# Graph attention with a gated FFN on one Trainium2 core: when scan results are transposed back, and when the first node's destination terms are copied

## The chip, the core and the metric

The kernel runs as one program on 1 core of a Trainium2 chip. The metric is device time in microseconds (us) of one execution, from its own record. Five engines run their own instruction lists in order and meet through semaphores: PE (TensorE; PEld is its weight load), DVE (VectorE), ACT (ScalarE), POOL (GpSimd) and SP (SyncE, which here only issues DMA).

## The reference

One layer of a relational graph attention network, then a feed-forward network with four experts, of which two count per node.

```python
feat_all = einsum('ni,rhid->rnhd', layernorm(x), conv_weights)   # 30000 nodes, 8 relations, 4 heads, 64
feat_src_e = feat_all[edge_type, src]                            # 510000 edges, sorted by dst
e = leaky_relu(sum(feat_src_e * attn_l[edge_type], -1) + sum(feat_all[edge_type, dst] * attn_r[edge_type], -1))
m = segment_max(e, dst)
ex = exp(e - m[dst])
alpha = ex / segment_sum(ex, dst)[dst]
x = x + segment_sum(alpha[..., None] * feat_src_e, dst).reshape(30000, 256) + h_bias
x = x + ffn(layernorm(x))      # shared 256-256-128-256, plus the 2 best of 4 experts 256-128-64-256, by a softmax gate
```

All data are float32. The edges come sorted by destination, 17 per node on average.

## The kernel before

**Two stages.** The first stage (up to about 1800 us) computes the features of every node and relation and stores them in DRAM, and works out lists and records of the edges. The second stage (about 1800 us to the end) is the one that the change touches. A third part, a slow path for unusual graphs, has loops that run zero times here.

**Blocks.** The second stage goes through 253 blocks of edges (`t` from 0 to 252; 2048 edges each, as 128 partitions x 16 units, neighbours overlapping). A block's feature rows are partly read back from a staged array and partly fetched by indirect DMAs from POOL (`gather`, L1152, 12 to 13 per block). Each block belongs to at most 128 nodes.

**What a block goes through.** By the names in the code:

- `dest_nodes` (DVE, L1164) makes a one-hot matrix, `dest_rows_of` (PE, L1172) multiplies it with the nodes' destination terms into PSUM tile `pe`: for each partition the terms of up to 4 nodes that its edges can belong to.
- `dest_first` (ACT, L1177) copies the first node's terms from `pe` to all 16 units of the tile `ere`. `dest_next` (DVE, L1182, three instructions) overwrites them where a unit belongs to the second, third or fourth node. `dest_types` (DVE, L1189) picks the relation.
- `scores` (DVE, L1206 to L1213) adds source and destination terms and takes the maxima `tops` of runs within a partition.
- `turn_ends` (PE, L1219) transposes `tops` into PSUM tile `t1`. `across` (DVE, L1225 and L1226) runs two scans over the partitions and writes the maxima of neighbours into `car`. `turn_back` (PE, L1232) multiplies `car` with a small constant and so fetches the scan results back, transposed, into PSUM tile `t2`. `t1` and `t2` share one PSUM buffer.
- `softmax` (DVE, L1238 to L1243) reads `t2` and subtracts the maxima; `exps` (ACT, L1248 and L1249) takes the exponentials and copies them beside the features.
- `onehot` (ACT, L1199 and L1200, three units at a time) makes the one-hot matrices of edges to nodes; `weigh` (DVE, L1256) multiplies features by exponentials; `sums` (PE, L1263) adds up per node; `finish` (DVE, L1329 to L1333) divides and adds the input. `keep` stores the rows.

**The experts.** Finished nodes go through the feed-forward network in groups of 512 (`Experts`). A group's work is a list of 23 steps, one of which is issued in each slot (below): normalise (`spread` L918 with a table load on ACT, `scale` L928), transpose (`turn`, PE L936, copied out on ACT L938 as `xT`), the gate (L944), the first, second and third layers (L1000, L1047, L1068 to L1071). What follows a step on ACT or DVE is issued one slot later, as `after`. A group begins in every fourth block, and at times in the fifth.

**The order is written out by hand.** Under `tc.manual_schedule()` (L1338) nothing reorders instructions: a loop over `t` and over six slots `c` issues everything, and each engine runs its part in that order. In iteration `t`, by slot:

- slot 0: DMAs of block `t+3`, gathers of `t+1`, store of `t-3`; `weigh` of `t-2`; `softmax` and `exps` of `t-1`
- slot 1: `scores` of `t`; `dest_first` of `t+1`, behind the experts' step and its `after`
- slot 2: `turn_ends` of `t`; two `dest_next` of `t+1`
- slot 3: `across` of `t`, the third `dest_next`, `dest_nodes` of `t+2`
- slot 4: `turn_back` of `t`; `finish` of `t-2`
- slot 5: `dest_rows_of` of `t+2`; `dest_types` of `t+1`
- in every slot: one chunk of `weigh` and, at the end, one experts' step with the former step's `after`, one chunk of `onehot` of `t-1` and one chunk of `sums` (of `t-2` in slots 0 to 2, of `t-1` in slots 3 to 5).

## Time and profile before

| what | value |
|---|---|
| median of 3 runs | 6114.72 us (6105.19 to 6117.77) |
| profiled execution, own time | 6111.61 us |
| its span (first to last instruction) | 6109.9 us |
| PE busy | 5621.0 us, 92% |
| PEld busy | 3559.5 us, 58% |
| DVE busy | 4519.3 us, 74% |
| ACT busy | 3396.1 us, 56% |
| POOL busy | 3983.9 us, 65% |
| mean granted TensorE clock | 0.954 of full speed |

The profiled execution is 3.1 us under the median of the runs, and its time is 1.7 us over its span. Shares of busy time are means over both stages. From 2300 to 5900 us the second stage runs evenly: in each 400 us PE is busy for 360 to 370 us, DVE for 353 to 357, ACT for 272 to 279, POOL for 289 to 296. All four engines are in use most of the time and wait for one another in turn, so the time is read from who waits for whom inside a block, and not from these shares.

### The profile page before, as it was taken

The page shows a single profiled execution, that of the slowest core. Times are in us where ns is not written, and L with a number is a line of the kernel's source. Part 1 is how long each engine was busy: PE and PEld are TensorE (multiplying, and loading weights), DVE is VectorE, ACT ScalarE, POOL GpSimd, SP SyncE. Part 2 cuts the span into 40 slices and gives each one's busy share as a digit, 9 for nine tenths or more (in the row PEclk, how much of TensorE's full clock was granted, in tenths as well). Part 3 has the DMA queues.
Part 4 walks back from the last instruction along what each step waited for, and adds up shares of the span by engine and source line. Part 5 has one row for each costly group of instructions (what it writes and reads, how often), then busy time and mean ns, then how long its engine had stood idle before and what let it go on. Part 6 is the DMA issues. An engine that isn't in the chain of part 4 may idle for free. (4 is left out here: it accounts for less than half of the span.)

```text
span 6109.9 us, 88666 instructions
## 1 busy us (share of the span) xinstructions
PE 5621.0 (92%) x20369; PEld 3559.5 (58%) x20370; DVE 4519.3 (74%) x13102; ACT 3396.1 (56%) x8847; POOL 3983.9 (65%) x4455
## 2 busy tenths in 40 slices
PE   8899999999987999999899999889999989999997
PEld 4455555555545666666666666666666666666664
DVE  6575333333339888888888888888898888888883
ACT  3343222222226667667666676767666666666763
POOL 1035666666666777777777777777777777777770
PEclk9999999999998999999999999999999999999998
DMA  8568999999997666666666666666666666666651
GB/s 193 137 243 274 355 364 358 356 356 354 356 321 208 179 182 182 184 184 177 180 183 181 182 180 182 181 181 178 182 189 180 181 180 180 182 178 180 184 169 35
DMA packets 847971, 1315.89 MB, mean 215 GB/s; under 512 B 226577, under 2 KB 646053, under 8 KB 817221
## 3 DMA queue, kind: packets, MB, share of 16 engines
q1 hardware_dynamic: 587476, 710.74, 35.5%
q0 software_dynamic: 194400, 539.40, 31.4%
q10 hardware_dynamic: 65552, 59.93, 3.0%
q8 instruction: 169, 2.77, 0.2%
q14 instruction: 374, 3.06, 0.2%
HBM read 855.54 MB, written 454.06 MB: 214 GB/s over the span
## 5 line engine op out<-in xcount | busy, mean ns | idle before, releaser
L1152 POOL DMA_INDIRECT ft<-feat,rk x3154 | 3021.0, 958 | 1133.5 <-issue 418.2
L1263 PE MATMUL po<-ft,oh 128*128 128x260 f32 x8100 | 2181.3, 410 | 23.6 <-ACT oh L1200 22.9
L1263 PEld LDWEIGHTS po<-ft,oh 128*128 128x128 f32 x8100 | 1546.4, 200 | 609.7 <-issue 255.2
L368 PE MATMUL ps<-w,xT 128*128 128x448 f32 (+1 forms) x4700 | 1717.3, 520 | 25.4 <-ACT fo L370 16.6
L1199 ACT ACTIVATE oh<-icol,rk 128x128 f32<-128x128 f32 x4050 | 1333.6, 390 | 0.0
L368 PEld LDWEIGHTS ps<-w,xT 128*128 128x128 f32 x4700 | 875.8, 191 | 723.3 <-issue 606.7
L1256 DVE TENSOR_TENSOR ft<-ft,p 128x768 f32<-128x768 f32 x1518 | 1285.6, 855 | 5.1 <-ACT ft L1249 5.0
L803 POOL DMA_INDIRECT fr<-feat,lists x896 | 851.1, 950 | 428.1 <-issue 235.1
L370 ACT COPY fo<-ps 128x448 f32<-128x448 f32 (+1 forms) x830 | 427.6, 521 | 1203.4 <-PE ps L368 850.6
L1200 ACT ACTIVATE oh<-oh 128x384 f32<-128x384 f32 x1518 | 740.3, 488 | 49.3
L1182 DVE COPY_PREDICATED ere<-rk,pe 128x512 f32<-128x512 int16 (+1 forms) x759 | 554.0, 730 | 187.6 <-ACT ere L1177 170.8
L1248 ACT ACTIVATE p<-e 128x64 f32<-128x64 f32 (+1 forms) x253 | 71.1, 281 | 796.9 <-DVE e L1243 796.4
L370 DVE COPY fo<-ps 128x256 f32<-128x256 f32 x345 | 180.0, 522 | 440.8 <-PE ps L368 415.0
L1000 PE MATMUL ph<-xT,v 128*128 128x512 f32 (+2 forms) x960 | 450.6, 594 | 0.8 <-ACT h L1001 0.8
L357 DVE COPY xT<-ptr 128x256 f32<-128x256 f32 x170 | 71.9, 423 | 319.3 <-PE ptr L355 319.1
L1189 DVE COPY_PREDICATED ere<-rk,ere 128x256 f32<-128x256 int16 (+1 forms) x759 | 247.0, 325 | 17.5
L1000 PE MATMUL ph<-xT,w 128*128 128x512 f32 (+2 forms) x480 | 259.2, 666 | 0.0
L1232 PE MATMUL t<-ways,car 36*128 36x8 f32 x506 | 98.4, 265 | 174.7 <-DVE car L1226 174.7
L1070 PE MATMUL pf<-v,a 128*128 128x256 f32 x940 | 243.8, 382 | 4.9 <-DVE a L1055 4.9
L1000 PEld LDWEIGHTS ph<-xT,v 128*128 128x128 f32 x960 | 175.1, 193 | 124.1 <-issue 114.2
L1232 PEld LDWEIGHTS t<-ways,car 36*128 36x128 f32 x506 | 77.8, 192 | 267.6 <-issue 262.9
L1001 ACT ACTIVATE h<-ph,b 128x512 f32<-128x512 f32 (+2 forms) x180 | 121.0, 672 | 197.7 <-PE ph L1000 190.5
(241 smaller groups left out, 5806.9 us busy)
## 6 DMA issues: line engine op xcount, KB each, us to landing
feat<-fo SPq DMA_DIRECT2D x234, 1040.0 KB
ft<-stage SPq DMA_DIRECT2D x160, 390.0 KB
stage<-fr SPq DMA_DIRECT2D x448, 130.0 KB
stage<-fr ACTq DMA_DIRECT2D x448, 130.0 KB
ft<-feat,rk POOLq DMA_INDIRECT x3154
ft<-stage SPq DMA_DIRECT2D x80, 520.0 KB
xt<-in_x_dram SPq DMA_DIRECT2D x253, 128.0 KB
x_d<-xt SPq DMA_DIRECT2D x252, 128.0 KB
```

What stands on the lines that cost most here:

```text
L368: nc.tensor.matmul(ps, t["xT"][:, k, :], w[:, k, c0:c1], start=k == 0, stop=k == 1)
L370: eng(t["fo"][:, h0:h1, :HD], ps[:, :n].rearrange("p (a d) -> p a d", d=HD))
L803: nc.gpsimd.indirect_dma_start(out=fr, out_offset=None, in_=feat[0:min(early(i // GI * GI) * P, N) * R, :], in_offset=bass.IndirectOffsetO ...
L1000: nc.tensor.matmul(ps[:, :self.w], lhs, rhs, start=i == 0, stop=i == len(pairs) - 1)
L1070: nc.tensor.matmul(pf[:M], self.a2[:, i, tok], v3[:, i, :], start=False, stop=False)
L1152: nc.gpsimd.indirect_dma_start(out=s.ft[:, u].rearrange("p h d -> p (h d)"), out_offset=None, in_=feat[:, :], in_offset=bass.IndirectOffse ...
L1182: nc.vector.copy_predicated(s.ere, s.mask[:, k - 1, :, None].to_broadcast(at), s.pe[:, k:k + 1].to_broadcast(at))
L1189: nc.vector.copy_predicated(s.ere[:, :, :n], s.bits[:, i, :, None].to_broadcast([P, s.u, n]), s.ere[:, :, n:2 * n])
L1199: nc.scalar.activation(s.oh[:, u, :], icol, AF.Abs, bias=s.nd[:, u:u + 1])
L1200: nc.scalar.activation(s.oh[:, u0:u1], s.oh[:, u0:u1], AF.Relu, bias=1.0, scale=-1.0)
L1256: nc.vector.tensor_mul(fc, fc, pc[:, :, None].to_broadcast([P, (u1 - u0) * H, HD]))
L1263: nc.tensor.matmul(s.po.rearrange("n h d -> n (h d)"), s.oh[:, u, :], s.ft[:, u].rearrange("p h d -> p (h d)"), start=u == 0, stop=u == s. ...
```

## The change

`turn_back` of a block is issued in slot 5 in place of slot 4. On PE it so comes after the experts' step and the chunk of `sums` of slot 4, and just ahead of `dest_rows_of`. `dest_first` of the next block is issued in slot 0 in place of slot 1. On ACT it so comes ahead of the `onehot` chunk of slot 0 and ahead of the `after` of slot 1. No instruction is added or taken away, none has another shape, and no DMA is moved.

```diff
@@ -1356,7 +1356,7 @@
                             nc.sync.dma_start(*outs.pop(0))
                     if c == 2:
                         at(turn_ends, t)
-                    if c == 4:
+                    if c == 5:
                         at(turn_back, t)
                     if c == 5:
                         at(dest_rows_of, t + 2)
@@ -1388,7 +1388,7 @@
                                 late.append(after)
                         for after in ready:
                             after()
-                    if c == 1:
+                    if c == 0:
                         at(dest_first, t + 1)
                     at(onehot, t - 1, c)
                     at(sums, t - 1 - (c < 3), (c - 3) % NCH)
```

## The prediction

> **What bounds the kernel now.** The chain that ended last on the page holds only an idle loop's instruction, so I read the waits of the steady part (2100 to 5900 us): waiting instruction, releaser, total us, times, longest.

> ```profile
> ACT p L1248 <- DVE e L1243: 708.9, 225, 9.1
> ...
> DVE ere L1182 <- ACT ere L1177: 160.2, 107, 2.2
> PE t L1232 <- DVE car L1226: 159.7, 70, 2.8
> ...
> DVE car L1225 <- PE t L1219: 95.5, 120, 1.9
> ```

> The second and third are the two waits that the change goes for. Each falls in few blocks, so I followed the timeline block by block. The experts' 23 steps give a cycle of four kinds of block: norm (holds L918, L928, L936), gate (L944, then the first layer), expert (second layer), last (L1068 to L1071). Between the start of the run and its end I count 55 cycles from one norm block to the next: 38 of four blocks, 17 with one more block, without experts' steps, behind the last block. One norm block, first on DVE, then PE, then ACT (start, us, engine, line, operation, idle time before it and releaser):

> ```profile
> 4110.57 0.94 DVE L1256 TENSOR_TENSOR ft<-ft,p 128x768 f32<-128x768 f32 x1
> 4113.09 1.49 DVE L1182 COPY_PREDICATED ere<-rk,pe 128x512 f32<-128x512 int16 x2 [1.58 <-ACT ere L1177]
> ```

> ```profile
> 4111.65 1.58 PE L1263 MATMUL po<-ft,oh 128*128 128x260 f32 x6 [0.63 <-ACT oh L1200]
> 4116.03 0.36 PE L1232 MATMUL t<-ways,car 36*128 36x8 f32 x2 [2.80 <-DVE car L1226]
> 4116.32 0.66 PE L936 MATMUL ph<-ident,c_xn 128*128 128x128 f32 x4
> 4116.81 2.36 PE L1263 MATMUL po<-ft,oh 128*128 128x260 f32 x6
> ```

> ```profile
> 4107.91 0.28 ACT L1248 ACTIVATE p<-e 128x64 f32<-128x64 f32 x1 [8.00 <-DVE e L1243]
> ...
> 4112.49 0.56 ACT L1177 COPY ere<-pe 128x512 f32<-128x512 f32 x1
> ...
> 4120.91 1.28 ACT L1248 ACT_TABLE_LOAD   x1
> 4123.30 0.28 ACT L1248 ACTIVATE p<-e 128x64 f32<-128x64 f32 x1 [1.10 <-DVE e L1243]
> ```

> DVE sets the pace here: PE waits for it for 2.80 us, and ACT for 8.00 us before and 1.10 us behind a stretch without a gap. In the gate block PE then waits for xT from ACT (L938, 1.48 us at 4124.42). From there through the expert block to L1219 of the last block PE has no wait, and DVE waits for PE at L1225 (0.7 to 0.9 us in each expert block, 0.2 to 0.8 in each last one). So a cycle is: DVE from the last block's L1225 to the gate block's L1243, ACT's L1248, L1249, L938, then PE.

> The TensorE clock belongs to PE's part. Four stretches (us, busy PE PEld DVE ACT POOL with counts, granted clock, DMA share, GB/s):

> ```profile
> 4113.90:4117.30 3.40, 1.27 (x9) 1.22 (x10) 3.36 (x7) 3.34 (x10) 2.49 (x4) 0.99 0.37 94
> 4117.30:4120.70 3.40, 3.40 (x13) 2.92 (x12) 3.26 (x12) 3.30 (x10) 2.49 (x4) 0.50 0.84 187
> ...
> 4188.90:4192.30 3.40, 2.12 (x17) 2.06 (x18) 3.30 (x8) 3.12 (x10) 2.56 (x3) 1.00 0.58 176
> 4192.30:4195.70 3.40, 3.40 (x9) 1.66 (x8) 3.19 (x9) 2.36 (x8) 2.72 (x3) 0.51 0.41 104
> ```

> A stretch of 3.41 us with little streamed through PE is followed by one at half clock: the first pair lies in the norm block, behind the 2.80 us wait, where PE has time; the second in the gate block, behind the xT wait and the 4-column L944, where PE has none. Cycles of four blocks last 65.77, 67.39 and 69.02 us with 0, 1 and 2 half-clock stretches in PE's part, so each costs 1.62 us. Over the 55 cycles they are none in 24, one in 21, two in 10: 41 in all, 66 us.

> **dest_first one slot earlier.** No instruction is added: 253 copies of 0.57 us. In the norm block the copy can start at 4110.17, behind L918, and end at 4110.7; DVE is free at 4111.51, so its wait of 1.58 us goes. Over 55 norm blocks these waits are 89.1 us. But DVE is then met by ACT. ACT works without a gap from 4107.91 to the end of the table load at 4122.19, and the order inside does not change its sum. So L1248 at 4123.30 can come earlier only by its own wait, 1.10 us (1.056 mean, 58.1 us over 55), and with it xT and PE's part. I take 58 and not 89.

> The other 75 us of that wait lie in expert blocks (0.6 to 2.2 us each). There L1225 comes next and waits for PE: its 0.91 us becomes up to 2.8. Worth nothing, as PE's part has no gap.

> What the copy is moved past: `onehot` chunk 0 comes 0.57 us later. In the norm block PE's 0.63 us wait for it becomes 1.20, hidden by the 2.80 us wait behind; without that cover 0.57 x 55 = 31 us. Elsewhere PE uses that chunk only in slot 3, microseconds after it is made. No DMA or POOL instruction is issued from the moved lines.

> **turn_back one slot later.** 253 times two matmuls, 0.39 us. In the norm block PE no longer stands 2.80 us for `car`: it goes to L936, which needs ACT's second pair of L928 (end 4115.48), so it starts at 4115.5 in place of 4116.32 and reaches `turn_back` about 1.9 us later, when `car` (now ready near 4114.3) has long been there. This saves PE time before the xT wait, which ACT ends: worth nothing directly.

> The cost is in DVE, which needs the result for L1238. Such a wait is absent from the trace; its size follows from these starts at the end of a gate block (the third is the expert block that follows):

> ```profile
> 4070.50 0.18 DVE L1238 TENSOR_TENSOR c<-t,rk 128x32 f32<-128x32 f32 x1
> ```

> ```profile
> 4067.84 0.39 PE L1232 MATMUL t<-ways,car 36*128 36x8 f32 x2
> 4071.29 0.38 PE L1172 MATMUL pe<-er,ohb 128*128 128x128 f32 x2
> ```

> ```profile
> 4080.31 0.41 DVE L1225 TENSOR_TENSOR_SCAN car<-through,t 4x127 f32<-4x127 f32 x1 [0.91 <-PE t L1219]
> ```

> The result lands 2.27 us before L1238 wants it; the new place ends where L1172 starts, 3.06 us later. So L1238 waits about 0.8 us. 31 of the 55 gate blocks are like this (mean 0.81, 25 us in all); in the others there are 3.7 us to spare. Queued behind L1238 are DVE's `scores` and the whole expert block, and ACT's L1248, but DVE has 0.91 + 1.9 us to spare there before L1225, and what PE needs of ACT (the second layer's input) is 6 us ahead. So I cost it at nothing, and at 25 us if that cover is gone. At the end of the last block 1.35 us of 1.81 are used, of the expert block 3.06 of 3.42, of the norm block about 2.6 of 5.2: no wait.

> **The clock.** The norm block's hole in PE, 0.63 + 2.80 us around three sums, becomes about 1.2 and 1.8: it trips the half clock less often. That sounds good, but a norm block at full clock brings PE to the xT wait sooner. In the 10 cycles without a half-clock stretch there the xT wait is 3.1 us in place of 1.4, and all 10 have two half-clock stretches in PE's part. With xT 1.1 us earlier the wait would be about 2. Bounds: all 41 stretches go (-66 us), or every cycle has two (110 - 41 = 69, +112 us). I take one per cycle, 55 - 41 = 14 more, +23 us, between the two kinds of row.

> [...] The rows above trip on a gap of 2.80 us and on 1.46 us of waiting beside 4-column matmuls. [...]

> **Sum.** 6111.6 (profiled execution) - 58 + 23 = 6076.6; the median lies 3.1 above it: 6080. POOL sets a floor: it stands idle beyond its usual 0.3 us per gather for only 130 us over the blocks from the 15th on, so no more than about 130 us can be won.

> **Rivals.**

> - *The clock's stretches shrink.* xT comes earlier and PE's holes are shorter, so PE's part may see fewer: from 6057 (still 41) to 6114.7 - 58 - 66 = 5991 (none). For it: 24 cycles have none now. Against: the 10 cycles with a fast norm block.
> - *Half clock in PE's part, twice per cycle (slower).* If the norm block now always runs at full clock, the xT wait and L944 fill a stretch in each cycle: 6114.7 - 58 + 112 = 6169. It decides from 36 more stretches on (58 / 1.62), 1.4 per cycle. For it: those 10 cycles, all with two. Against: their xT wait was 3.1 us, not 2.
> - *The gain is spent elsewhere.* L1238's 25 us and the 31 us of the later one-hot chunk are not covered: 6114.7 - 58 + 56 = 6113. Against: 2.8 us of room on DVE in the expert block and the hole on PE in the norm block.
> - *The waits only change their names:* ACT is the limit at once and 0 of the 58 is left, 6115. Against: the 1.10 us wait is there in all 55 cycles.

> **How the numbers follow.** About 0.2% (12 us) is what a measurement of this kernel can tell from no change. Forecast (6057 to 6100) 0.45; fewer stretches 0.25; gain spent or only renamed 0.14; two stretches per cycle, or well on the way there, 0.16. Faster by over 0.2% are the first two and a little of the third: 0.72; within 0.2%: 0.13; slower: 0.15. The range goes down to the middle of the second case, 6024, and up through the third to a quarter of the last, 6125.

> **What would show it.** Right: L1182's wait for L1177 nearly gone (from 160 us to under 20), L1232's for L1226 under 30, L1225's for L1219 up to some 170 as expert blocks wait for PE in its place; L1248 behind the norm block without its 1.1 us; L1238 with a new wait for L1232 of some 25 us; cycles of 64.7, 66.3 or 67.9 us. Wrong: an L1182 wait that stays; a norm block whose ACT stretch grows beyond 14.3 us; an L1238 wait after which L1225 of the expert block no longer waits; or cycles of four blocks mostly at 67.9 us or above, which would be the clock.

## The result, and the profile after

| | us |
|---|---|
| before, median of 7 runs | 6113.95 (6097.06 to 6117.77) |
| after, median of 7 runs | 6138.55 (6134.09 to 6143.47) |
| ratio after / before, 95% interval | 1.0047 (1.0035 to 1.0059) |
| after, profiled execution, its span | 6136.24, 6134.5 |

The change makes the kernel 24.6 us slower. The profiled executions differ by the same 24.6 us (6136.24 against 6111.61), so they can be compared part by part.

The waits of the steady part, kernel after (2100 to 5900 us; waiting instruction, releaser, total us, times, longest):

```profile
ACT p L1248 <- DVE e L1243: 695.3, 174, 8.4
...
DVE car L1225 <- PE t L1219: 235.8, 153, 2.2
...
PE pg L944 <- ACT xT L938: 135.0, 53, 2.6
...
DVE c L1238 <- PE t L1232: 53.9, 69, 1.6
...
PE ph L936 <- ACT c_xn L928: 52.0, 87, 1.1
```

The line of the kernel before for xT, same view:

```profile
PE pg L944 <- ACT xT L938: 85.2, 47, 3.3
```

Of the two waits that the change went for, L1182's for L1177 (160 us before) is gone, and L1232's for L1226 (160 us before) is down to 4.9 us. In their place L1225 waits 236 us for PE in place of 95, L1238 has a wait that it did not have, and PE waits for xT in every cycle (135 us in place of 85). The kernel got rid of two waits in the norm block, and PE comes later to the blocks behind it.

One norm block with the start of its gate block, timeline of the kernel after, first ACT, then PE (start, us, engine, line, operation, idle time before it and releaser):

```profile
4178.27 0.28 ACT L1248 ACTIVATE p<-e 128x64 f32<-128x64 f32 x1 [8.00 <-DVE e L1243]
...
4191.26 1.28 ACT L1248 ACT_TABLE_LOAD   x1
4192.55 0.28 ACT L1248 ACTIVATE p<-e 128x64 f32<-128x64 f32 x1
```

```profile
4185.40 0.33 PE L936 MATMUL ph<-ident,c_xn 128*128 128x128 f32 x1 [1.10 <-ACT c_xn L928]
...
4186.05 1.48 PE L1263 MATMUL po<-ft,oh 128*128 128x260 f32 x6
4187.46 0.39 PE L1232 MATMUL t<-ways,car 36*128 36x8 f32 x2
...
4190.73 0.28 PE L944 MATMUL pg<-gw,xT 128*128 128x4 f32 x2
4193.62 3.15 PE L944 MATMUL pg<-gw,xT 128*128 128x4 f32 x14 [2.60 <-ACT xT L938]
```

ACT's L1248 behind the norm block starts without its wait of 1.1 us, as forecast, and ACT is the limit there now. PE's hole of 2.80 us ahead of L1232 has gone: L936 and six matmuls of `sums` come first. But PE then reaches L944 early and stands 2.60 us for xT. The same place by stretches of 3.40 us (us, busy PE PEld DVE ACT POOL with counts, granted clock, DMA share, GB/s):

```profile
4183.90:4187.30 3.40, 2.13 (x11) 1.40 (x9) 3.29 (x11) 3.34 (x10) 2.67 (x3) 1.00 0.45 113
4187.30:4190.70 3.40, 3.40 (x20) 2.96 (x19) 3.26 (x10) 3.34 (x10) 2.60 (x3) 1.00 0.93 222
4190.70:4194.10 3.40, 0.80 (x6) 0.68 (x5) 3.23 (x8) 3.31 (x8) 2.49 (x4) 0.92 0.83 280
4194.10:4197.50 3.40, 3.40 (x15) 3.30 (x16) 2.97 (x8) 2.83 (x9) 2.70 (x3) 0.50 0.46 120
4197.50:4200.90 3.40, 3.40 (x9) 1.83 (x9) 1.20 (x3) 1.14 (x4) 2.58 (x3) 0.58 0.41 102
4200.90:4204.30 3.40, 3.40 (x11) 1.85 (x11) 3.16 (x12) 1.43 (x5) 2.49 (x4) 1.00 0.48 125
```

The first row is the norm block's hole, now too full to bring a half-clock stretch: the second row stands at 1.00. The third row is the xT wait with PE busy for 0.80 of 3.40 us. Two stretches at half clock follow, not one. Most of the first is L944 itself: 14 of its 16 matmuls, of 4 columns each, keep PE "busy" for 3.15 us and stream 56 columns in all, and the second half-clock stretch follows.

**Where the 24.6 us are.** The second stage is cut into the same 55 cycles as before. PE's part of a cycle runs from L944 of the gate block to L1219 of the last block, and a half-clock stretch is one step of 3.413 us at 0.50 in the clock's own records.

| half-clock stretches in PE's part | cycles before | cycles after | us, four blocks, before / after | us, five blocks, before / after |
|---|---|---|---|---|
| none | 24 | 0 | 65.77 / - | 80.09 / - |
| one | 21 | 12 | 67.39 / 66.31 | 81.78 / 80.62 |
| two | 10 | 43 | 69.02 / 67.90 | 83.36 / 82.24 |

Cycles of one kind are 1.1 us shorter, as forecast. But the kinds have changed: 98 stretches (12 + 86) in place of 41, each at 1.6 us. 55 x 1.056 = 58 us are won and 57 x 1.62 = 92 us lost, +34; the mean cycle says 71.41 to 71.99, +0.58 x 55 = +32 us. The other -7 us lie outside these cycles, 6.3 of them ahead of the 15th block's softmax (2032.59 before, 2026.31 after); what they come from stays open.

The length of the xT wait does not settle alone whether a cycle has one stretch or two: after the change 12 cycles with a wait of 2.5 to 2.6 us have one, and 40 with 2.3 to 2.6 us have two. In the traces of before and after every change of the clock lies on a fixed grid of 3.413 us. In the 12 cycles PE restarts behind the xT wait 0.66 to 2.13 us after a line of this grid, in all 43 others outside that range. Ahead of PE's part half clock costs nothing that shows: in the kernel before, four-block cycles with no stretch in PE's part have 2.7 such stretches there in the mean, those with two have none, and 1.62 us for each one in PE's part fits both.

### The profile page after: what moved, and what is told of

It reads as the page before. It is cut to its first block, busy times and chain, and to the rows that moved or that the text cites. A ratio compares the mean times of both kernels' runs of the same rounds, so it can differ in the third digit from the quotient of the medians.

```text
span 6134.5 us, 88626 instructions
## 1 busy us (share of the span) xinstructions
PE 5660.2 (92%) x20369; PEld 3558.2 (58%) x20370; DVE 4519.3 (74%) x13102; ACT 3398.0 (55%) x8847; POOL 3988.0 (65%) x4455
## 5 line engine op out<-in xcount | busy, mean ns | idle before, releaser
L1263 PE MATMUL po<-ft,oh 128*128 128x260 f32 x8100 | 2154.2, 407 | 60.1 <-ACT oh L1200 45.2
L1263 PEld LDWEIGHTS po<-ft,oh 128*128 128x128 f32 x8100 | 1545.3, 200 | 656.2 <-issue 237.5
L1256 DVE TENSOR_TENSOR ft<-ft,p 128x768 f32<-128x768 f32 x1518 | 1286.1, 855 | 2.4 <-ACT ft L1249 2.4
L1200 ACT ACTIVATE oh<-oh 128x384 f32<-128x384 f32 x1518 | 740.3, 488 | 48.1
L1182 DVE COPY_PREDICATED ere<-rk,pe 128x512 f32<-128x512 int16 (+1 forms) x759 | 552.4, 728 | 21.1 <-ACT ere L1177 4.4
L1248 ACT ACTIVATE p<-e 128x64 f32<-128x64 f32 (+1 forms) x253 | 71.1, 281 | 804.9 <-DVE e L1243 804.3
L944 PE MATMUL pg<-gw,xT 128*128 128x4 f32 x940 | 162.7, 296 | 143.6 <-ACT xT L938 143.6
L1225 DVE TENSOR_TENSOR_SCAN car<-through,t 4x127 f32<-4x127 f32 x253 | 101.6, 402 | 251.0 <-PE t L1219 250.7
L1000 PE MATMUL ph<-xT,w 128*128 128x512 f32 (+2 forms) x480 | 271.6, 694 | 0.0
L944 PEld LDWEIGHTS pg<-gw,xT 128*128 128x128 f32 x940 | 163.0, 255 | 152.7 <-ACT xT L938 149.4
```

What stands on the lines that cost most here:

```text
L944: nc.tensor.matmul(pg[:M, t, :], self.xT[:, k, t * M:(t + 1) * M], gw[:, k, :], start=k == 0, stop=k == 1)
L1000: nc.tensor.matmul(ps[:, :self.w], lhs, rhs, start=i == 0, stop=i == len(pairs) - 1)
L1182: nc.vector.copy_predicated(s.ere, s.mask[:, k - 1, :, None].to_broadcast(at), s.pe[:, k:k + 1].to_broadcast(at))
L1200: nc.scalar.activation(s.oh[:, u0:u1], s.oh[:, u0:u1], AF.Relu, bias=1.0, scale=-1.0)
L1256: nc.vector.tensor_mul(fc, fc, pc[:, :, None].to_broadcast([P, (u1 - u0) * H, HD]))
L1263: nc.tensor.matmul(s.po.rearrange("n h d -> n (h d)"), s.oh[:, u, :], s.ft[:, u].rearrange("p h d -> p (h d)"), start=u == 0, stop=u == s. ...
```

## The experiments

Two theories. **Clock:** the freed waits move PE's idle time from the norm block, where half clock costs nothing, to the xT wait, where it costs 1.6 us a stretch. **Late fetch:** `turn_back` one slot later makes DVE late at L1238 (53.9 us of waits) and the cycle with it. A kernel's ratio is to the kernel before, run on the same chip, with its 95% interval. Except where "after" is named, the edits are made to the kernel before.

### One half of the change at a time

`e1_turn_back_only`:

```diff
-                    if c == 4:
+                    if c == 5:
                         at(turn_back, t)
```

> Only turn_back moves (slot 5); dest_first stays in slot 1. Clock theory (the new order closes PE's hole in the norm block, PE comes sooner to the wait for xT, and PE's part of the cycle gets more half-clock stretches of 1.62 us): the 58 us of the earlier copy are missing, L1248 behind the norm block keeps its 1.05 us wait, cycles stay at 65.8 or 80.1 us plus 1.62 per stretch, and there are 60 to 110 stretches in place of 41: 6145 to 6225 us. Late-fetch theory (the loss is DVE's new wait for turn_back at L1238, 54 us in the steady part of the changed kernel): 41 stretches or so, L1238 waits for 25 to 54 us, and the cycles are longer by that: 6140 to 6195 us.

`e2_dest_first_only`:

```diff
-                    if c == 1:
+                    if c == 0:
                         at(dest_first, t + 1)
```

> Only dest_first moves (slot 0); turn_back stays in slot 4. Clock theory: cycles of 64.7 or 79.05 us plus 1.62 per half-clock stretch; PE's wait for car in the norm block falls from 2.8 to about 0.7 us, PE then waits for c_xn some 1.1 us, so the norm block is mostly at full clock here too and PE's part has 70 to 98 stretches: 6100 to 6148 us. Late-fetch theory: no wait at L1238, 41 stretches, 6114 - 58 = 6056 us.

Measured: e1 6198.78 us, ratio 1.0153 (1.0139 to 1.0166); e2 6146.01 us, ratio 1.0060 (1.0046 to 1.0073). Waits of e1, then of e2 (2100 to 5900 us):

```profile
PE pg L944 <- ACT xT L938: 181.2, 52, 4.0
...
DVE ere L1182 <- ACT ere L1177: 142.5, 104, 1.6
```

```profile
DVE car L1225 <- PE t L1219: 291.7, 156, 3.5
...
PE pg L944 <- ACT xT L938: 151.6, 53, 3.0
```

e2 has the old `turn_back` and no wait of L1238 at all, and is slower all the same, with 105 half-clock stretches in PE's part. So late fetch falls as the cause. Its four-block cycles of 66.35 us (one stretch) and 67.89 us (two) are those of the kernel after. In e1 the L1182 wait and ACT's 1.06 us stay, so nothing is won: its four-block cycles last 67.39 us with one stretch, as before, 68.96 with two and 69.90 with three, of which the first begins while PE still stands for xT. That makes 108 stretches in place of 41, or the worth of about 100 if only what lies behind the xT wait is counted. L1238's waits (40.8 us in e1) do not show in the cycles with one stretch. Either half alone is enough to bring PE to the xT wait early. Put together they lose less than e1 alone because the 58 us of `dest_first` are real.

### Filling the xT wait

`e3_fill_xT_wait` is the kernel after with three matmuls that compute nothing, into a tile that nobody reads, ahead of L944 (the trace shows each as two records):

```diff
+if todo and getattr(todo[0], "__name__", "") == "gates":
+    hole = ph_p.tile([P, TM], F32, name="ph")
+    for _f in range(3):
+        nc.tensor.matmul(hole, ident, v1.rearrange("p e k f -> p (e k f)")[:, :TM], start=True, stop=True)
```

> The changed kernel with three more matmuls (identity by 512 columns of the first experts' weights, into an unread PSUM tile) issued on PE ahead of the gate matmuls L944, 3 x 0.86 us in the 2.6 us wait for xT. Clock theory: the idle window before PE's part is gone, 98 half-clock stretches fall to 0 to 30, and 1.62 us come back for each: 5980 to 6030 us. Late-fetch theory, or any in which the waits themselves cost the time: unchanged or slower by what does not fit in the wait, 6138 to 6160 us.

Measured: 5984.12 us, ratio 0.9795 (0.9782 to 0.9809). PE on the timeline, then the stretches (columns as above); L1388 is the filling:

```profile
2937.99 2.36 PE L1263 MATMUL po<-ft,oh 128*128 128x260 f32 x10
2940.18 2.74 PE L1388 MATMUL ph<-v,ident 128*128 128x512 f32 x6
2942.76 1.97 PE L944 MATMUL pg<-gw,xT 128*128 128x4 f32 x16
```

```profile
2939.40:2942.80 3.40, 3.40 (x13) 1.85 (x11) 3.16 (x11) 3.31 (x8) 2.48 (x4) 1.00 0.69 228
2942.80:2946.20 3.40, 3.40 (x24) 2.89 (x23) 3.30 (x7) 3.34 (x10) 2.49 (x4) 1.00 0.42 113
```

No wait of L944 for L938 is left, and of the 98 stretches in PE's part none. The cycles last 64.72 and 79.04 us: 1.05 us less than before's undisturbed 65.77 and 80.09, which is the gain that the prediction gave to `dest_first` (1.056 us). The mean granted clock of the whole run goes from 0.953 to 0.979. More work on PE, all of it useless, makes the kernel 2.5% faster than it was with the change alone.

### Real work in its place

`e4_sums_before_gate` is the kernel after with two chunks of `sums` (those of slots 1 and 2) issued ahead of the gate's matmuls; nothing is added:

```diff
+if c == 1 and t < NBLK and todo and getattr(todo[0], "__name__", "") == "gates":
+    for i in range(2):
+        at(sums, t - 2, 4 + i)
+        ahead_of_gate.append(1 + i)
...
+if c in ahead_of_gate:
+    ahead_of_gate.remove(c)
+else:
     at(sums, t - 1 - (c < 3), (c - 3) % NCH)
```

> The changed kernel, where in slot 1 of a gate block the sums chunks of slots 1 and 2 (5 units, 2.6 us of PE) are issued ahead of the gate matmuls, so that PE works while it waits for xT. Clock theory: PE's part is 2.6 us shorter in each cycle (143 us over 55) and loses most of its half-clock stretches (up to 90 us); POOL's floor and DVE cut this off: 5970 to 6020 us. Late-fetch theory: L1238 comes later on DVE or as before, 6110 to 6140 us.

Measured: 5956.02 us, ratio 0.9754 (0.9740 to 0.9767), 14 us below the range that was expected. It beats both kernels; e11 (below) cannot be told from it, and nothing in this study is faster. Its waits (2100 to 5800 us):

```profile
POOL ft L1152 <- issue: 334.2, 1097, 0.3
POOL ft L1152 <- PE po L1263: 226.7, 744, 0.3
...
DVE e L1206 <- DMA ft<-feat,rk: 62.2, 56, 3.3
...
PE pg L944 <- ACT xT L938: 22.5, 52, 1.4
```

35 stretches remain in PE's part. Ahead of a gather POOL no longer waits longer than 0.5 us for anything, and nearly always 0.3 us, its usual gap (before: up to 3.5 us); DVE now waits 62 us for the gathered rows at L1206, in place of 1.0 us before. By these waits the next limit, the gathers on POOL, has been reached.

### The reverse test: filling the hole of the kernel before

If full holes are what makes the kernel slow, the kernel before must become slower when its norm-block hole is filled with work that fits into it. `e5_before_fill_norm_hole` and its repeat `e9_before_fill_norm_hole` put two filling matmuls ahead of `turn_back` in the norm block:

```diff
+if c == 4 and t < NBLK and len(todo) == 18:
+    hole = ph_p.tile([P, TM], F32, name="ph")
+    for _f in range(2):
+        nc.tensor.matmul(hole, ident, v1.rearrange("p e k f -> p (e k f)")[:, :TM], start=True, stop=True)
```

> The kernel before, with two more matmuls (identity by 512 columns, 2 x 0.86 us, into an unread PSUM tile) ahead of turn_back in each norm block, inside PE's 2.8 us wait for car; nothing else moves. Clock theory: the norm block no longer falls to half clock, PE comes to the xT wait sooner and waits 3 us there in every cycle, and PE's part gets two half-clock stretches per cycle, as in the ten cycles of before with a fast norm block: 41 become 90 to 110, and the kernel is slower by work that fits in a wait, 6190 to 6225 us. Any theory without the clock: the work is hidden, 6105 to 6120 us.

> The kernel of e5 again, on a chip where the kernel before takes its 6110 us. Clock theory: two half-clock stretches in PE's part of every cycle (90 to 110 in place of 41), slower by work that fits in a wait: 6190 to 6225 us. Any theory without the clock: the work is hidden, 6105 to 6120 us.

e5 ran on a chip on which the kernel before itself took 7006.13 us. The profile of e5 has gaps on PE, DVE, ACT and POOL (the longest of each 4.2 to 14.4 us) that nothing in it explains, such as these (2400 to 6500 us):

```profile
ACT p L1248 <- issue: 404.6, 51, 14.4
```

There e5 took 7017.35 us, ratio 1.0019 (1.0006 to 1.0033). That says nothing of the theory either way, so all four kernels of that series were repeated on a chip where the kernel before takes 6105.99 us. e9, the repeat: 6208.47 us, ratio 1.0164 (1.0146 to 1.0181). Its waits (2100 to 5800 us):

```profile
DVE ere L1182 <- ACT ere L1177: 172.8, 102, 2.8
...
PE pg L944 <- ACT xT L938: 157.7, 51, 3.4
...
PE t L1232 <- DVE car L1226: 67.8, 60, 1.6
```

The hole (L1232 for L1226) shrinks from 155 us (before, same window) to 68; DVE's wait at L1182 grows a little (173 us, 156 before), and the kernel is 102 us slower. In 48 of the 55 norm blocks PE still waits for `car` behind the filling, so nearly all of the added work is hidden. In PE's part lie 107 stretches, or the worth of about 99 behind the xT wait, as many as after the change. Four-block cycles with one stretch last 67.40 us, as before (67.39), those with two 68.72, so the cycles are longer by their stretches alone: hidden work cost 1.6%, through the clock. This is the part of the change that went wrong, done without the change.

### What each half is worth once the clock is out of the way

`e6_turn_back_fill_xT`, repeat `e10_turn_back_fill_xT`: the edit of e1 with the filling of e3.

> Only turn_back moved (as in e1), with the three filling matmuls ahead of L944 (as in e3). Clock theory: no half-clock stretch in PE's part, cycles of 65.8 and 80.1 us as in the 24 cycles of before without one, though L1238 waits for turn_back: about 6040 us (6030 to 6055). If the late fetch costs time of its own, the cycles are longer than 65.8 and 80.1 by up to 0.8 us: up to 6085 us.

> The kernel of e6 again. Clock theory: no half-clock stretch in PE's part, cycles of 65.8 and 80.1 us though L1238 waits for turn_back: about 6040 us (6030 to 6055). If the late fetch costs time of its own, the cycles are longer by up to 0.8 us: up to 6085 us.

e6 (chip of e5): 7000.98 us, 0.9995 (0.9982 to 1.0008). e10: 6091.99 us, ratio 0.9973 (0.9962 to 0.9984). This missed its expectation of about 6040: three fillers are too few when xT comes late, and the xT wait of L944 is still 0.84 us in the mean, so 26 stretches remain. Read by kinds of cycle it still answers: cycles without a stretch last 65.94 and 80.22 us, against 65.77 and 80.09 before. So `turn_back`'s later slot by itself costs at most 0.13 to 0.17 us a cycle, some 8 us; the cycles of e1 with one stretch show no cost.

`e7_dest_first_sums_before_gate`, repeat e11: the edit of e2 with the order of e4. `e8_before_sums_before_gate`, repeat e12: the order of e4 alone.

> Only dest_first moved (as in e2), with the sums chunks of slots 1 and 2 ahead of the gate matmuls (as in e4). turn_back is in its old place. If the move of turn_back is worth nothing, the same as e4: 5945 to 5970 us. If it helps once PE works in the xT wait, this is slower than e4 by 10 us or more.

> The kernel of e7 again. If the move of turn_back is worth nothing, the same as e4: 5945 to 5970 us. If it helps once PE works in the xT wait, slower than e4 by 10 us or more.

> The kernel before, with the sums chunks of slots 1 and 2 ahead of the gate matmuls; neither line of the change. The xT wait is 1.4 us in most cycles here, so some 1.2 us of the sums stick out; ACT's 1.05 us wait behind the norm block stays; POOL's floor is near. Clock theory: most of the 41 stretches go and PE's part is 1.4 to 2.6 us shorter, 5960 to 6020 us, slower than e4 by the rest of dest_first's 58 us that POOL leaves. If the clock were not the point: 6110 - 55 x 1.4 = 6033 us or above.

> The kernel of e8 again: before, with two sums chunks ahead of the gate matmuls. Clock theory: most of the 41 stretches go and PE's part is 1.4 to 2.6 us shorter, 5960 to 6020 us, slower than e4 by the rest of dest_first's 58 us that POOL leaves. If the clock were not the point: 6033 us or above.

e7 and e8 (chip of e5): 7023.08 us, 1.0028 (1.0012 to 1.0044), and 7027.01 us, 1.0028 (1.0011 to 1.0045). The repeats: e11 5964.05 us, ratio 0.9762 (0.9746 to 0.9779); e12 5976.68 us, ratio 0.9786 (0.9770 to 0.9802). e11 cannot be told from e4, so `turn_back`'s move is worth nothing that shows here either. e12 has nearly all of the gain without any part of the change: 11 stretches, and most four-block cycles at 64.66 us. `dest_first` adds some 13 us to it (the intervals of e11 and e12 overlap), and not its 58. Two things in the traces stand against it, and no run parts them: DVE's L1206 waits 68.4 us for the gathers in e11, 0.8 us in e12, and 44 stretches remain in e11 to 11 in e12.

## Why the prediction was wrong

- *`dest_first`, -58 us:* right. Undisturbed cycles went from 65.77 and 80.09 to 64.72 and 79.04 us (e3), 55 x 1.05 us. L1182's wait fell to nothing (forecast under 20), and what was won is ACT's 58 us and not the 89 of DVE's wait.
- *The expert blocks' 75 us reappear at L1225:* right. In the expert blocks L1225's wait grew from 45.6 to 116.5 us, by 71. In all 235.8 us were measured against "up to some 170", because PE is also later by the extra half-clock stretches: in e3, without them, it is 143.6.
- *`turn_back`, costed at nothing, 25 us of waits at L1238 covered:* near enough. The waits are 53.9 us. 43 of them lie ahead of expert blocks whose L1225 still waits 2.1 us, and come with the extra half-clock stretches (0.2 us of them are left in e3); the other 11 are 17 waits of 0.65 us at the end of an expert block, where the prediction saw none. The bare cost is at most 8 us by e10.
- *The later one-hot chunk:* PE's wait for it grew to 1.11 us (forecast 1.20) and stayed hidden, right.
- *The clock, +23 us:* this step failed, by its size. "I take one per cycle ... between the two kinds of row": it is one per cycle in 12 cycles and two in 43, 57 more in place of 14, +92 us in place of +23. With it the prediction's own sum gives 6111.6 - 58 + 92 = 6146 against 6136 of the profiled execution, and 7 of these 10 us lie outside the cycles.

What was misjudged inside that step can be named. The hole in the norm block was forecast to shrink to about 1.2 and 1.8 us; it shrank further, to 1.11 and 1.10 us around the sums and L936. It was seen that this trips the half clock less often. The consequence was already in the trace of before, in the 10 cycles with a norm block at full clock: all 10 had two stretches. I weighed their xT wait of 3.1 us against a forecast of "about 2" and went halfway. It measured 2.6 us in most cycles, and of these most have two stretches. Nor is "about 2" a safe place for one per cycle: the three cycles of the kernel after with a wait of 1.74 to 1.82 us have two as well. The clock's records hold 1.00 and 0.50 and nothing between, and whether a cycle of the kernel after had one stretch or two went with how PE's restart lay on the grid (0.66 to 2.13 us behind a line of it, or outside that range), which the prediction did not ask. The rival "half clock in PE's part, twice per cycle" was the right mechanism, and its deciding point (36 more stretches) was passed with 57; at 6169 it was too dear, as 12 of the cycles have one and 7 us were won outside the cycles. The text's sign for being wrong, "cycles of four blocks mostly at 67.9 us or above, which would be the clock", is what the profile shows: 31 of 38 at 67.90.

Gaps of 2.60 us (after), 2.80 and 1.46 us (before) were followed by half clock here, while in 17 cycles of the kernel before xT waits of 1.4 to 1.5 us were not; the length of a gap alone did not tell.

## What to carry to other kernels

Where PE's clock falls after a stretch of little work, as in these runs, a wait that PE has anyway can be worth keeping, and one that is removed must be followed to the place where the idle time goes: in the part with time to spare half clock cost nothing that showed here, in the part that sets the pace 1.6 us each. Look for that place first and put work that is ready into it, by order alone if possible; e12 gained 2.1% by that alone, while two moves that each took away real waits lost 0.5%. And where a cost comes in steps, a value between two rows of the trace stands for no cycle: find the level at which the step lies, as below, and count on which side of it the new order falls.
